# Two attention layers on one core: 64x128 products in place of 64x64 quadrants, and another order at the end of a batch

## The chip, the core and the metric

The kernel runs on one core of a Trainium2 chip. The metric is the device time of one execution in microseconds; the kernel before takes 5070.74 us (median of three runs, 5064.38 to 5071.53). The profile shown here is of an execution with a span of 5060.0 us. The engines are called PE (TensorE, the matrix engine; its weight loads are listed apart as PEld), DVE (VectorE), ACT (ScalarE), POOL (GpSimd) and SP (SyncE, which issues most of the transfers). All data are 32-bit floats.

## What is computed

The input is an array of 8 images, 512 channels by 1024 positions. Two layers of attention with residuals run one after the other. Layer 0 is ordinary attention of 8 heads with 64 channels each, and the change leaves it alone. Layer 1, cut to what matters:

```python
q, k, v = (einsum("oc,bct->bot", w, gn(x)) for w in (w_q, w_k, w_v))  # 8 heads of 64
attn = einsum("bhdq,bhdT->bhqT", q, k) * scale           # "scores"
attn = einsum("gh,bhqT->bgqT", w_head, attn)             # "mixing": heads are mixed
attn = softmax(attn, axis=-1)
mean, var = attn.mean((-2, -1)), attn.var((-2, -1))      # one pair a batch and head
attn = (attn - mean) / sqrt(var + EPS) * in_gamma + in_beta
out = einsum("bhqT,bhdT->bhqd", attn, v)                 # "values"
x = x + w_proj @ out + b_proj
```

Mixing stands between the scores and the exponential, so it must be done on all 8 heads' scores of a query and key. The division by the softmax's sum, and the normalisation over a whole head (the "instance" statistics), are applied to the result instead of to the 1024 x 1024 weights: the kernel needs sums of e and of e squared for each query and head, and scales `out` with them.

## The kernel before

The order of the instructions on each engine is the order in which the program emits them (a manual schedule), and each engine takes its queue in order. Waits between engines are put in by the framework where data or buffers demand them.

Layer 1 works through the batches one by one. One batch has 4 query blocks of 256 queries and 4 key blocks of 256 keys, so 16 blocks `t`, and two *half-steps* `x` for each: `half_step` (L1302 on) is called for x = 0 to 36. In a half-step x below 32 the scores of four heads are made, in two parts `i`; mixing lags four half-steps behind (`y = x - MLAG`), and squares, sums and values lag five (`w = y - 1`). So in the steady part, x = 5 to 31, PE does in this order: scores part 0, mix j = 0 and 1, scores part 1, values.

- `scores(x, i)` (L1117) makes 2 heads x 256 queries x 256 keys into a PSUM tile of two banks, index m (the head) choosing the bank. The tile `s` has one buffer; for x below 4 two of three parts use the tiles `m` instead, of which there are two. The result is copied to `raw` in SBUF (L1126 by DVE, L1128 by ACT), one of the two being chosen by i and x.
- `regroup(t)` (L1137), after an odd x, sends `raw` to eight tiles `re` by SP's transfers, so that the heads of one query come to lie on neighbouring partitions.
- `mix(y, j)` (L1150) multiplies pieces of `re` as the stationary operand with the constant `wmix`, 64 columns: 32 products for each j, 8 tiles `re` (R_ORDER) by 2 halves of the keys (`c`) by 2 halves of the partitions (`a`). The result is in a tile `m`; ACT takes its exponential (L1156). `c` selects the half of the output's partitions, `a` the partitions of the inputs and the PSUM bank.
- `squares` (L1166, ACT), `sum_e` and `sum_e2` (L1171, L1173, L1177, DVE) gather the sums.
- `values(w)` (L1195) adds to two accumulators in PSUM.
- After every eighth values block, `totals` (L1221) sums over the keys with a product by ones, PE; the rows are copied by DVE and ACT (L1232, L1230) and brought to a compact form `c` by two transfers (L1236). `leave` (L1210, L1212) copies the accumulators out. `reciprocals` (L1244 to L1264) inverts the sums, sends them to DRAM (`zd`, L1246) and back, broadcast to all partitions (`rzb`, L1249), and adds up the squares; `divide` (L1270) multiplies by `rzb`. For the first three query blocks the last two are run 2 and 5 half-steps later, from an agenda.
- While half-steps 32 to 35 run, two `k_half` each (L1004) make the next batch's keys.

After the last half-step come `leave`, the first pair of the next batch's V projection (`v_pair`, PE, L1021, copied by ACT L1025 and then DVE L1026), the flushed agenda with `reciprocals` and `divide` of the last query block, `instance` (which sums the squares, L1276 and L1278, spreads the sum by a small product `pi` on PE, L1280, and takes an inverse root by a chain of small DVE operations, L1282 to L1292), the second V pair, `affine` for 8 heads (L1298 ACT, L1300 DVE), the output product (L1083) and the next batch's queries (L1053). `small_psum1` and `v_pair` both take their PSUM from the two buffers of `m`.

Of the kernel before, what the change touches and what calls it, by code (L numbers as in the profile page):

```python
# [18 lines left out]
P = 128  # L19
# [448 lines left out]
def tile_two_attention_layers(  # L468
# [19 lines left out]
    nc = tc.nc  # L488
    B, C, T = x_d.shape
    H = w_head.shape[0]  # L490
    D = C // H
# [24 lines left out]
    def const_tile(name, shape, dt=F32):  # L516
        return const.tile(shape, dt, tag=name, name=name)
# [13 lines left out]
    ones = const_tile("ones", [P, P])  # L531
# [12 lines left out]
    wmix = const_tile("wmix", [P, H, Q8])  # L544
# [26 lines left out]
    NQB = 4  # L571
# [78 lines left out]
    with ExitStack() as l0:  # L650
# [42 lines left out]
        for oc in range(3 * NCC):  # L693
            for c in range(NCC):
                nc.tensor.matmul(
                    pbq[:, oc : oc + 1], w0[:, c, ts(oc, P)], gnb[:, c : c + 1],
                    start=(c == 0), stop=(c == NCC - 1),
# [5 lines left out]
        n_t, xa_t, q_t, k_t, v_t = {}, {}, {}, {}, {}  # L703
# [187 lines left out]
        for b in range(B):  # L891
            ag = Agenda()
# [25 lines left out]
    with ExitStack() as l1:  # L918
# [16 lines left out]
        KB = 2 * P  # L935
# [4 lines left out]
        MLAG = 4  # L940

        def m_psum(nm):
            return ps_m.tile([P, 2, FB], F32, tag="m", name=nm)

        def small_psum1(nm):
            return m_psum(nm)[:, 0]

        y_t, qo_t, k_t, v_t, w_t = {}, {}, {}, {}, {}
# [64 lines left out]
        def v_pair(b, i):  # L1013

            if i == 0:
                v_t[b] = kvpool.tile([P, NT, C], F32, tag="v", name=f"v1_{b}")
            ps = m_psum(f"pv1_{b}_{i}")
            w = w_t["v", b]
            for m in range(2):
                for c in range(NCC):  # L1020
                    nc.tensor.matmul(  # L1021
                        ps[:, m], y_t[b][:, c, ts(2 * i + m, P)], w[:, c],
                        start=(c == 0), stop=(c == NCC - 1),
                    )
            nc.scalar.copy(v_t[b][:, 2 * i], ps[:, 0])  # L1025
            nc.vector.tensor_copy(v_t[b][:, 2 * i + 1], ps[:, 1])  # L1026
# [71 lines left out]
        class Attention1:  # L1098
# [4 lines left out]
            def scores(self, x, i):  # L1103

                b, t, hp = self.b, x // 2, x % 2 * 2 + i
                qb, kb = t // NKB, t % NKB
                nm = f"s1_{b}_{x}_{i}"
                if x < MLAG and (2 * x + i) % 3:
                    ps = m_psum(nm)
                else:  # L1110
                    ps = ps_s.tile([P, 2, FB], F32, tag="s", name=nm)
                pv = ps.rearrange("p m (j k) -> p m j k", j=2)
                for j in range(2):
                    for c in range(2):
                        for m in range(2):
                            r = slice(m * D, m * D + D)
                            nc.tensor.matmul(  # L1117
                                pv[c * D : c * D + D, m, j],
                                qo_t[b][r, 2 * qb + j, hp, ts(c, D)],
                                k_t[b][r, hp, ts(kb, KB)], start=True, stop=True,  # L1120
                            )
                if x % 2 == 0 and i == 0:
                    self.raw[t] = rawpool.tile([P, H, 2, KB], F32, tag="raw", name=f"raw_{b}_{t}")
                dst = self.raw[t][:, 2 * hp : 2 * hp + 2]
                if i == 0 and (x < MLAG or x % 2 == 0):
                    nc.vector.tensor_copy(dst, pv)  # L1126
                else:
                    nc.scalar.copy(dst, pv)  # L1128
# [10 lines left out]
            def mix(self, y, j):  # L1139

                t, kc = y // 2, y % 2
                if j == 0:
                    self.e[y] = epool.tile([P, 2, T], F32, tag="e", name=f"e1_{self.b}_{y}")
                ps = m_psum(f"m1_{self.b}_{y}_{j}")
                for r in R_ORDER:
                    for c in range(2):
                        k0 = kc * P + c * D
                        for a in range(2):
                            rows = slice(a * D, a * D + D)
                            nc.tensor.matmul(  # L1150
                                ps[c * D : c * D + D, a, ts(r, D)],
                                self.re[t, r][rows, j, k0 : k0 + D],
                                wmix[rows].rearrange("p g i -> p (g i)"),
                                start=True, stop=True,
                            )
                nc.scalar.activation(self.e[y][:, j], ps.rearrange("p a c -> p (a c)"), AF.Exp)  # L1156

            def squares(self, y, j):
# [113 lines left out]
            def instance(self):  # L1272

                b = self.b
                s = stat.tile([P, 1], F32, tag="is", name=f"is_{b}")
                nc.vector.reduce_sum(s, self.s2, axis=AX.X)  # L1276
                sb = stat.tile([P, H], F32, tag="isb", name=f"isb_{b}")
                nc.vector.tensor_scalar_mul(sb, blk8, s)  # L1278
                ps = small_psum1(f"pi_{b}")
                nc.tensor.matmul(ps[:, :H], ones, sb, start=True, stop=True)  # L1280
                var = stat.tile([P, H], F32, tag="ivar", name=f"ivar_{b}")
                nc.vector.tensor_scalar(  # L1282
                    var, ps[:, :H], 1.0 / (T * T), EPS - 1.0 / (T * T), ALU.mult, ALU.add
                )
                r = rsqrt(stat, var, f"i_{b}", H)
                self.A = stat.tile([P, H], F32, tag="iA", name=f"iA_{b}")
                nc.vector.tensor_mul(self.A, r, gam8)
                self.cv = stat.tile([P, H], F32, tag="icv", name=f"icv_{b}")
                nc.vector.scalar_tensor_tensor(
                    self.cv, self.A, -1.0 / T, bet8, ALU.mult, ALU.add  # L1290
                )
                nc.vector.tensor_mul(self.cv, self.cv, vs[:, :, b])  # L1292
# [9 lines left out]
            def half_step(self, x, ag):  # L1302
                y, w = x - MLAG, x - MLAG - 1
                if 0 <= w - 1 < NX and w % QLAG == 0:
                    self.leave((w - 1) // QLAG)
                if 0 <= w < NX:
                    self.squares(w, 0)
                    self.sum_e(w, 0)
                if x < NX:
                    self.scores(x, 0)  # L1310
                if 0 <= w < NX:
                    self.squares(w, 1)
                    self.sum_e(w, 1)
                    self.sum_e2(w, 0)
                    self.sum_e2(w, 1)
                if 0 <= y < NX:
                    self.mix(y, 0)
                    self.mix(y, 1)
                if x < NX:
                    self.scores(x, 1)  # L1320
                    if x % 2:
                        self.regroup(x // 2)
                if 0 <= w < NX:
                    self.values(w)
                    self.e.pop(w)
                    if w % QLAG == QLAG - 1:
                        qb = w // QLAG
                        self.totals(qb)
                        ag.at(x + 2, lambda: self.reciprocals(qb))
                        ag.at(x + 5, lambda: self.divide(qb))  # L1330
                ag.run(x)


# [15 lines left out]
        for b in range(B):  # L1349
            more = b + 1 < B  # L1350
            a = Attention1(b)
            ag = Agenda()
            for i in range(NV):
                ag.at(1, lambda i=i: v_pair(b, NV + i))
            if more:
                for c in range(NCC):
                    ag.at(6 + 2 * c, lambda c=c: load_y(b + 1, [c]))
                    ag.at(14 + 2 * c, lambda c=c: load_w(("k", b + 1), wkT, [c]))
                    ag.at(22 + 2 * c, lambda c=c: load_w(("v", b + 1), wvT, [c]))
                    ag.at(24 + c, lambda c=c: normalize1(b + 1, [c]))  # L1360
                for i in range(2 * NCC):
                    ag.at(NX + i // 2, lambda i=i: k_half(b + 1, i))
            for x in range(NX + MLAG + 1):
                a.half_step(x, ag)

            a.leave(NQB - 1)
            if more:
                v_pair(b + 1, 0)
            ag.flush()
            a.instance()  # L1370
            if more:
                load_w(("q", b + 1), wqT)
                v_pair(b + 1, 1)
            for g in range(H):
                a.affine(g)
            for oc in range(NCC):
                out1(b, oc)
            if more:
                for oc in range(NCC):
                    q_chunk(b + 1, oc)  # L1380
# [69 lines left out]
```

## Time and profile before

| | busy us | share of the span | instructions |
|---|---|---|---|
| PE | 4542.6 | 90% | 58392 |
| PEld | 2440.7 | 48% | 58392 |
| DVE | 2643.7 | 52% | 3082 |
| ACT | 2008.8 | 40% | 2161 |
| POOL | 271.7 | 5% | 139 |

Layer 0 fills the time up to about 2050 us, layer 1 the rest, some 373 us a batch. Each product of 32-bit floats stands in the trace as two matmuls and two weight loads, so that the counts are twice the program's. A busy time is the union of the instructions of a group; the mean that follows it is the length of one, and since several run at once on different parts of the array, the sum of the lengths is larger. "Idle before" is the idle time of the engine just before the instructions of a group, with what ended it; "issue" means that nothing in the profile explains it. A form like `64*64 64x256` reads: 64 rows and 64 columns of weights, and an output of 64 partitions by 256 columns. In the tables by window the columns are the length, the busy time and count of PE, PEld, DVE, ACT and POOL, the granted PE clock, the share of the DMA engines and GB/s. Matmuls may be missing from a trace, a few per cent at most, and their ends are modelled, so that starts are the better measure.

### The profile page before, as it was taken

The page shows a single profiled execution, that of the slowest core. Times are in us where ns is not written, and L with a number is a line of the kernel's source. Part 1 is how long each engine was busy: PE and PEld are TensorE (multiplying, and loading weights), DVE is VectorE, ACT ScalarE, POOL GpSimd, SP SyncE. Part 2 cuts the span into 40 slices and gives each one's busy share as a digit, 9 for nine tenths or more (in the row PEclk, how much of TensorE's full clock was granted, in tenths as well). Part 3 has the DMA queues.
Part 4 walks back from the last instruction along what each step waited for, and adds up shares of the span by engine and source line. Part 5 has one row for each costly group of instructions (what it writes and reads, how often), then busy time and mean ns, then how long its engine had stood idle before and what let it go on. Part 6 is the DMA issues. An engine that isn't in the chain of part 4 may idle for free.

```text
span 5060.0 us, 128186 instructions
## 1 busy us (share of the span) xinstructions
PE 4542.6 (90%) x58392; PEld 2440.7 (48%) x58392; DVE 2643.7 (52%) x3082; ACT 2008.8 (40%) x2161; POOL 271.7 (5%) x139
## 2 busy tenths in 40 slices
PE   7999999999999999988888888888888888888987
PEld 4343424242424243466366466466465465465464
DVE  1737373838283828266265266266275265265365
ACT  0414141404141414076176175165175265274274
POOL 1202020202020200000000000000000000000000
PEclk9999999999999999999999999999999999999999
DMA  1000000000000000265264264264274364363364
GB/s 67 1 33 1 34 1 34 1 33 1 34 1 34 1 17 0 84 173 129 64 178 121 76 170 119 81 164 119 85 177 102 101 163 100 100 174 99 100 149 111
DMA packets 205048, 408.68 MB, mean 81 GB/s; under 512 B 35024, under 2 KB 35024, under 8 KB 204496
## 3 DMA queue, kind: packets, MB, share of 16 engines
q1 hardware_dynamic: 203072, 396.19, 29.1%
q8 instruction: 458, 7.50, 0.7%
q10 hardware_dynamic: 1152, 4.19, 0.2%
q14 instruction: 94, 0.77, 0.1%
q0 software_dynamic: 272, 0.02, 0.0%
HBM read 97.54 MB, written 33.82 MB: 26 GB/s over the span
## 4 chain that ended last, share of the span: by engine, by line
PE 81%; DVE 6%; issue 5%; ACT 5%; DMA 2%; SPq 0%; DVEq 0%; ACTq 0%
PE a L1195 9%; PE s L1117 9%; PE s L820 8%; PE m L1150 8%; PE a L845 8%; PE pv L1021 5%; PE pp L1083 5%; PE pk L1004 5%; PE pk L768 4%; PE pq L1053 4%; PE pp L768 4%; PE pq L768 4%; PE pv L791 4%; PE t L1221 2%; ACT raw L1128 1%
## 5 line engine op out<-in xcount | busy, mean ns | idle before, releaser
L825 ACT ACTIVATE e<-s 128x1024 f32<-128x1024 f32 x512 | 498.6, 1022 | 568.2 <-PE s L820 557.2
L1150 PE MATMUL m<-wmix,re 64*64 64x64 f32 x32768 | 561.9, 219 | 123.1 <-issue 115.6
L1117 PE MATMUL s<-k,q 64*64 64x256 f32 x8192 | 575.7, 389 | 86.9 <-issue 48.1
L1150 PEld LDWEIGHTS m<-wmix,re 64*64 64x64 f32 x32768 | 544.2, 135 | 178.0 <-issue 140.1
L1173 DVE TENSOR_TENSOR z<-z,e 128x1024 f32<-128x1024 f32 x448 | 536.6, 1219 | 123.4 <-ACT e L1156 123.3
L1195 PE MATMUL a<-e,v 128*64 128x128 f32 x8192 | 550.9, 288 | 49.4 <-issue 49.4
L1156 ACT ACTIVATE e<-m 128x1024 f32<-128x1024 f32 x512 | 504.3, 1024 | 200.2 <-PE m L1150 199.4
L1177 DVE TENSOR_TENSOR z<-z,e 128x1024 f32<-128x1024 f32 x448 | 532.1, 1220 | 62.4 <-ACT e L1166 61.7
L1195 PEld LDWEIGHTS a<-e,v 128*64 128x64 f32 x8192 | 478.3, 144 | 161.7 <-issue 159.5
L820 PE MATMUL s<-q,k 64*128 64x512 f32 x2048 | 523.5, 629 | 2.3
L845 PE MATMUL a<-e,v 128*64 128x512 f32 x2048 | 495.2, 605 | 0.0
L1166 ACT ACTIVATE e<-e 128x1024 f32<-128x1024 f32 x448 | 461.5, 1069 | 0.0
L1128 ACT COPY raw<-s 128x1024 f32<-128x1024 f32 x368 | 373.7, 1015 | 198.4 <-PE s L1117 190.3
L833 DVE TENSOR_TENSOR zacc<-zacc,e 128x1024 f32<-128x1024 f32 x320 | 411.5, 1286 | 48.0 <-ACT e L825 24.2
L1117 PEld LDWEIGHTS s<-k,q 64*64 64x64 f32 x8192 | 288.7, 134 | 243.7 <-issue 113.0
L1126 DVE COPY raw<-s 128x1024 f32<-128x1024 f32 x144 | 176.3, 1224 | 308.4 <-PE s L1117 286.5
L820 PEld LDWEIGHTS s<-q,k 64*128 64x128 f32 x2048 | 178.3, 189 | 327.6 <-issue 168.4
L845 PEld LDWEIGHTS a<-e,v 128*64 128x64 f32 x2048 | 125.1, 136 | 343.8 <-issue 324.9
L858 DVE RECIPROCAL rz<-z 128x512 f32<-128x512 f32 x64 | 214.8, 3356 | 81.0 <-PE z L854 81.0
L1083 PE MATMUL pp<-q,wp 128*128 128x512 f32 x512 | 231.9, 615 | 21.5 <-DVE q L1300 16.8
L1021 PE MATMUL pv<-wv,y 128*128 128x512 f32 x512 | 243.9, 635 | 0.0
L1004 PE MATMUL pk<-y,wk 128*128 128x512 f32 x512 | 231.3, 606 | 5.9 <-DMA y<-x 5.9
(165 smaller groups left out, 3547.4 us busy)
## 6 DMA issues: line engine op xcount, KB each, us to landing
re<-raw SPq DMA_DIRECT2D x1024, 256.0 KB
x<-in_x_dram SPq DMA_DIRECT2D x32, 512.0 KB
x<-x SPq DMA_DIRECT2D x32, 512.0 KB
y<-x SPq DMA_DIRECT2D x32, 512.0 KB
rzb<-zd SPq DMA_DIRECT2D x64, 256.0 KB
xs<-x SPq DMA_DIRECT2D x32, 512.0 KB
out_dram<-xs SPq DMA_DIRECT2D x32, 512.0 KB
wk<-in_wkT_dram SPq DMA_DIRECT2D x32, 256.0 KB
```

Of the source, the lines that this page charges most:

```text
L768: nc.tensor.matmul(ps[:, f], w[:, c, o0 + oc * P : o0 + (oc + 1) * P], rhs[:, c, ts(f, FB)], start=(c == 0), stop=(c == NCC - 1),)
L820: nc.tensor.matmul(ps[:, m], k[r, hp, ts(kc, P)], q[r, hp, ts(f, FB)], start=True, stop=True,)
L825: nc.scalar.activation(e[i], ps, AF.Exp)
L845: nc.tensor.matmul(acc[g][m * D : m * D + D], v[:, kc, ts(2 * hp + m, D)], e[i][:, m], start=(kc == 0), stop=(kc == NG - 1),)
L1021: nc.tensor.matmul(ps[:, m], y_t[b][:, c, ts(2 * i + m, P)], w[:, c], start=(c == 0), stop=(c == NCC - 1),)
L1083: nc.tensor.matmul(ps[:, f], w[:, n, ts(oc, P)], out_view(b)[:, n, ts(f, FB)], start=(n == 0), stop=(n == NQB - 1),)
L1117: nc.tensor.matmul(pv[c * D : c * D + D, m, j], qo_t[b][r, 2 * qb + j, hp, ts(c, D)], k_t[b][r, hp, ts(kb, KB)], start=True, stop=True,)
L1150: nc.tensor.matmul(ps[c * D : c * D + D, a, ts(r, D)], self.re[t, r][rows, j, k0 : k0 + D], wmix[rows].rearrange("p g i -> p (g i)"), star ...
L1156: nc.scalar.activation(self.e[y][:, j], ps.rearrange("p a c -> p (a c)"), AF.Exp)
L1173: nc.vector.tensor_add(self.z[:, j], self.z[:, j], self.e[y][:, j])
L1177: nc.vector.tensor_add(self.z2[:, j], self.z2[:, j], self.e2[j])
L1195: nc.tensor.matmul(self.acc[w][j * D : j * D + D, s].rearrange("p (c i) -> p c i", i=Q8), v_t[b][:, kc, ts(g, D)], self.by_head(self.e[y][ ...
```

## The change

It has three parts, all in layer 1. Scores and mixing no longer split the output's partitions into two halves: a product takes 64 rows and 128 columns of weights in place of two with 64 columns, so that there are half as many instructions. The DVE's share of the evictions of scores in the steady part moves from even half-steps to odd ones, where only ACT evicted. At the end of a batch the last `reciprocals` comes directly after `leave`, ahead of the V pair, and `instance` is cut in two: the sums before the V pair, the product and the root after it; `divide` and `affine` follow, and the second V pair is emitted after them. The aim is fewer instructions on PE and a shorter chain between the last values and the output product.

```diff
                 for j in range(2):
-                    for c in range(2):
-                        for m in range(2):
-                            r = slice(m * D, m * D + D)
-                            nc.tensor.matmul(
-                                pv[c * D : c * D + D, m, j],
-                                qo_t[b][r, 2 * qb + j, hp, ts(c, D)],
-                                k_t[b][r, hp, ts(kb, KB)], start=True, stop=True,
-                            )
+                    for m in range(2):
+                        r = slice(m * D, m * D + D)
+                        nc.tensor.matmul(
+                            pv[:, m, j], qo_t[b][r, 2 * qb + j, hp],
+                            k_t[b][r, hp, ts(kb, KB)], start=True, stop=True,
+                        )
...
-                if i == 0 and (x < MLAG or x % 2 == 0):
+                if i == 0 and (x < MLAG or x % 2):
                     nc.vector.tensor_copy(dst, pv)
...
                 for r in R_ORDER:
-                    for c in range(2):
-                        k0 = kc * P + c * D
-                        for a in range(2):
-                            rows = slice(a * D, a * D + D)
-                            nc.tensor.matmul(
-                                ps[c * D : c * D + D, a, ts(r, D)],
-                                self.re[t, r][rows, j, k0 : k0 + D],
-                                wmix[rows].rearrange("p g i -> p (g i)"),
-                                start=True, stop=True,
-                            )
+                    for a in range(2):
+                        rows = slice(a * D, a * D + D)
+                        nc.tensor.matmul(
+                            ps[:, a, ts(r, D)], self.re[t, r][rows, j, ts(kc, P)],
+                            wmix[rows].rearrange("p g i -> p (g i)"),
+                            start=True, stop=True,
+                        )
...
                 nc.vector.tensor_scalar_mul(sb, blk8, s)
+                self.sb = sb
+
+            def instance_end(self):
+                b = self.b
                 ps = small_psum1(f"pi_{b}")
-                nc.tensor.matmul(ps[:, :H], ones, sb, start=True, stop=True)
+                nc.tensor.matmul(ps[:, :H], ones, self.sb, start=True, stop=True)
...
                         self.totals(qb)
-                        ag.at(x + 2, lambda: self.reciprocals(qb))
-                        ag.at(x + 5, lambda: self.divide(qb))
+                        if qb < NQB - 1:
+                            ag.at(x + 2, lambda: self.reciprocals(qb))
+                            ag.at(x + 5, lambda: self.divide(qb))
...
             a.leave(NQB - 1)
+            a.reciprocals(NQB - 1)
+            a.instance()
+            ag.flush()
             if more:
                 v_pair(b + 1, 0)
-            ag.flush()
-            a.instance()
+            a.instance_end()
+            a.divide(NQB - 1)
+            for g in range(H):
+                a.affine(g)
             if more:
                 load_w(("q", b + 1), wqT)
                 v_pair(b + 1, 1)
-            for g in range(H):
-                a.affine(g)
             for oc in range(NCC):
                 out1(b, oc)
```

## The prediction

> **What bounds the kernel now.** The slices of the page come first: TensorE (PE) is busy in tenths 8 or 9 all along, so I look for what its time in layer 1 is made of. The costliest groups, and the DMA queues for one line:
>
> ```profile
> L1150 PE MATMUL m<-wmix,re 64*64 64x64 f32 x32768 | 561.9, 219 | 123.1 <-issue 115.6
> L1117 PE MATMUL s<-k,q 64*64 64x256 f32 x8192 | 575.7, 389 | 86.9 <-issue 48.1
> L1195 PE MATMUL a<-e,v 128*64 128x128 f32 x8192 | 550.9, 288 | 49.4 <-issue 49.4
> ...
> q8 instruction: 458, 7.50, 0.7%
> ```
>
> Mixing (L1150), scores (L1117) and values (L1195) each take some 560 us, and before them PE stands idle for 115.6 + 48.1 + 49.4 = 213 us on "issue", which no semaphore explains. The timeline of PE over two half-steps of batch 3 shows where:
>
> ```profile
> 3288.69 1.09 PE L1117 MATMUL s<-k,q 64*64 64x256 f32 x16
> 3289.61 2.04 PE L1150 MATMUL m<-wmix,re 64*64 64x64 f32 x128
> 3291.47 1.05 PE L1117 MATMUL s<-k,q 64*64 64x256 f32 x16
> 3292.45 1.97 PE L1195 MATMUL a<-e,v 128*64 128x128 f32 x32
> 3294.34 1.09 PE L1117 MATMUL s<-k,q 64*64 64x256 f32 x16
> 3295.26 2.04 PE L1150 MATMUL m<-wmix,re 64*64 64x64 f32 x128
> 3297.12 0.61 PE L1117 MATMUL s<-k,q 64*64 64x256 f32 x7
> 3300.35 0.86 PE L1117 MATMUL s<-k,q 64*64 64x256 f32 x9 [2.62 <-issue]
> ```
>
> An undisturbed half-step is, start to start, 0.92 (scores) + 1.86 (mix) + 0.98 (scores) + 1.89 (values) = 5.65 us; PE waits for no eviction in it. But in the second one it halts within a score block, after 7 of 16 products. A half-step has 192 records of matmuls and as many weight loads, 384 instructions, 256 of them in the 1.86 us of the mix. In the trace's DMA records packets of the instruction queue (16 KB each: 7.50 MB / 458) start at 3297.81 and 3313.92 us, where PE has just halted (last start before the halt near 3297.4), and PE goes on about 1.4 us after each has landed; when PE starves they follow each other 3.6 us apart. So I read the halt as instruction fetch. The third view, windows, gives its side effect and a warning for later:
>
> ```profile
> 2102.20:2106.00 3.80, 3.80 (x130) 3.78 (x129) 0.69 (x1) 0.59 (x1) 0.00 (x0) 1.00 0.00 0
> 2106.60:2110.00 3.40, 3.40 (x6) 1.34 (x5) 0.00 (x0) 0.00 (x0) 0.00 (x0) 0.50 0.00 0
> 3284.60:3300.30 15.70, 13.13 (x384) 10.38 (x384) 10.30 (x9) 10.53 (x11) 0.00 (x0) 0.90 0.68 171
> ```
>
> The granted clock (third column from the right) falls with the halts. Counted from the first to the 27th values block of a batch (26 half-steps and three blocks of totals of 3.03 us), the timelines give 188.6 to 203.0 us, mean 196.2 for batches 0 to 6 and 190.9 for the last: 7.2 us a half-step, not 5.65. ACT has 5.5 us of work in one (L1156 504.3, L1166 461.5 + 68.6, L1128 373.7, over 256), DVE 5.0, so neither bounds it.
>
> Last, the end of a batch, PE and the DMA issues:
>
> ```profile
> 3155.76 1.97 PE L1195 MATMUL a<-e,v 128*64 128x128 f32 x32
> 3160.72 2.96 PE L1221 MATMUL t<-z,ones 128*32 128x512 f32 x8 [3.00 <-DVE z L1177]
> ...
> 3166.34 8.02 PE L1021 MATMUL pv<-wv,y 128*128 128x512 f32 x16
> 3184.03 0.56 PE L1280 MATMUL pi<-isb,ones 128*128 128x8 f32 x2 [9.66 <-DVE isb L1278]
> 3184.45 9.19 PE L1021 MATMUL pv<-wv,y 128*128 128x512 f32 x16
> 3196.05 1.52 PE L1083 MATMUL pp<-q,wp 128*128 128x512 f32 x3 [2.40 <-DVE q L1300]
> ...
> 3167.09 1.21 SPq L1236 DMA_DIRECT2D c<-row  x2
> 3175.90 0.33 SPq L1246 DMA_DIRECT2D zd<-rz  x1
> 3177.32 1.14 SPq L1249 DMA_DIRECT2D rzb<-zd  x2
> ```
>
> The reciprocals sit behind the eviction of the V pair on DVE, the little product pi behind the divide and its broadcast from DRAM, and the second V pair behind pi: 9.66 us idle, then a cold clock. From the last values block to the output product takes 38.8 us on average in batches 0 to 6, 24.4 in batch 7.
>
> **What the Trainium skill says.** "TensorE: Matmul & The Clock Gate", LDWEIGHTS: a load takes columns / 1.2 ns, whatever the rows: 53 ns for 64 columns, 107 for 128. The trace agrees:
>
> ```profile
> 2102.15 3.81 PEld L1038 LDWEIGHTS pvs<-ys,wv 128*64 128x64 f32 x128 [0.76 <-issue]
> 1005.27 0.30 PEld L820 LDWEIGHTS s<-q,k 64*128 64x128 f32 x4 [0.81 <-ACT e L825]
> ```
>
> 128 loads of 64 columns in two column halves, with products of only 8 columns, come as pairs 58.3 ns apart: load-bound, 53 + 5. The four loads of a layer 0 score (64 rows, 128 columns) span 0.30 us with 0.19 each, so the second pair starts 0.11 after the first, and two row halves load together. Same page, HAM clock gate: a window of 3.4 us with little activity halves the clock; here that followed the idle of 2.6 us and more, and the load-bound stretch at 2102 (the windows above). "Runtime: NRT & Kernel Launch", instruction fetch: blocks of 16 KiB, 256 instructions, boundaries "mostly hidden". The packets agree in size; hidden they are not where a block is used up in 1.9 us. "TensorEngine Tiling (Array Packing)": row tiles run in parallel if they write different PSUM banks; the layer 0 pairs do, and m and a index banks here too.
>
> **The change, part by part.**
> *Scores.* Half as many products, of 128 columns and 256 long. Pairs at the 215.5 ns that the quadrants show now, four pairs instead of four fours: the same 0.86 us; the first load of a block is exposed for 0.05 more. 0.97 + 0.98.
> *Mix.* 64 loads of 128 columns in 32 pairs, products of 64 columns. The product streams 53 ns, the load needs 107: load-bound, 107 + 5 = 112 ns a pair (bounds: 109, the first pair of layer 0; 165 if load and product of the same rows could not overlap, 107 + 53 + 5). I take 112, as the layer 0 pairs and the load-bound v_sums say: 32 x 0.1117 = 3.57 us instead of 1.86, +1.71. It is on PE's path.
> *Fetch.* A half-step falls to 224 instructions; the fastest stretch, the mix, uses 128 in 3.57 us, 36 per us, half of 256 in 3.6 us. The halts and their cold windows go. Half-step: 0.97 + 3.57 + 0.98 + 1.89 = 7.41 us.
> *Evictions.* The DVE eviction moves from even to odd half-steps. ACT then has 6.0 us in an even one (two exps, two squares, two copies) and 5.0 in an odd one, DVE 4.3 and 5.6: under 7.41, so nothing. Behind ACT's second copy waits the next score block, 1.89 us of values later; the copy ends about 2.3 us after the mix, the block starts at 2.87.
> *Sums per batch* (0 to 6). Steady part 26 x 7.41 + 3 x 3.03 = 201.8 against 196.2: +5.6. First mix to first values: 3.57, then two exps and a copy on ACT until 5.9, then 5.5: 11.4 against 9.1, +2.3. The last five half-steps, where the next keys' projection (7.1 us) stands between: four mixes of 3.79 with the drain. Now one takes 2.03 and three 2.56, 47.5 in all where nothing halts, which would be +5.4; the mean with halts is 50.05, so 52.9 is +2.8.
> *End of a batch.* The reciprocals no longer wait for the V pair: the trace of batch 7, where there is none, gives 1.86 us from the issue of c to them, 1.4 from zd to rzb, 4.7 to the divide. So isb is ready at 3170.2, under the first V pair. Pi follows that pair at once (3174.4). The second V pair now waits for the PSUM buffer of the first, free at 3175.7 after the copies by ACT and DVE. DVE: pi's chain 3.0 us to 3178.7, the divide to 3179.9 (broadcast landed 3175.4), two affines per engine to 3181.5, all beside the V pair, which ends PE's queue at 3182.9. New waits: DVE's reciprocals wait 1.9 us for c with only that copy queued behind, whose PE work lasts longer. The V copies now wait behind the affines, which PE needs only 6.9 us later. Tail 24.4 instead of 38.8 (one cold block of totals aside): -14.4, and the output product starts warm, 27.7 instead of 28.9: -1.2.
> Sum: 5.6 + 2.3 + 2.8 - 15.6 = -4.9, seven times: -34. Batch 7: 201.8 - 190.9 = +10.9, +2.6, +0.1, and a tail in which only instance and its root (4.1) move under the broadcast: +9.5. Total about -24: 5070.7 - 24 = 5046.
>
> **Rivals.**
> *Trade, 0.80:* the above, 5046. Two gains of different kind meet an equal loss. Each ns of the pair's spacing is 32 x 32 x 8 ns = 8 us; 109 gives 5024, 115 gives 5073; the tail is good for 20 either way.
> *Weight loads worse, slower, 0.11:* a spacing of 125 gives 4.0 us a mix, +0.43 x 256 = 110: 5155; 165 gives 5480. For it: mixing would stream products only half the time, and the load-bound stretch at 2102 was followed by half clock. Against: there products streamed a tenth of it.
> *Halts stay, slower, 0.02:* if they are not the fetch, 7.41 + 1.5: about 5360.
> *Loads of 64 rows cost half, faster, 0.07:* the mix stays at 1.9, ACT's 6.0 bounds the half-step: -1.4 x 256, 4690. Against: the 0.11 us of layer 0.
>
> **How the numbers follow.** In the first case faster by over 0.2% (10 us) has 0.70, within 0.18, slower 0.12. With the others: faster 0.63, same 0.15, slower 0.22. The range 4995 to 5120 takes in the first case with its bounds and a spacing of 120, and leaves out 0.2.
>
> **What would show it.** Mix blocks of x64 lasting 3.57 us start to start (1.9 or 5 refutes the loads); no "issue" before L1146 and L1116; values to values 7.4; clock 1.00 in the steady part; pi without a wait, and 24 us from the last values to the output product.

## The result, and the profile after

The changed kernel takes 5034.99 us (median of four runs, 5034.15 to 5035.81), the kernel before 5067.56 us in the same comparison (5061.06 to 5071.53). The ratio is 0.9937, with a 95% interval of 0.992 to 0.9954: 32.6 us faster. The prediction was 5046 us, between 4995 and 5120. The profiled spans are 5060.0 us before and 5033.6 us after.

The groups of the page of the changed kernel that answer to those shown of before, and the queue of the instructions (columns: busy time, mean ns of one, then the idle time before them and what ended it):

```profile
L1146 PE MATMUL m<-wmix,re 64*128 64x64 f32 x16384 | 946.7, 271 | 0.0
L1116 PE MATMUL s<-k,q 64*128 64x256 f32 x4096 | 559.4, 395 | 15.3 <-ACT raw L1126 8.9
L1190 PE MATMUL a<-e,v 128*64 128x128 f32 x8192 | 503.5, 276 | 0.0
...
q8 instruction: 298, 4.88, 0.4%
```

The 213 us of "issue" are gone from all three groups, as predicted; the scores cost about what they cost before (559.4 us busy, 575.7 with twice the instructions); and mixing, with half the instructions, is busy for 946.7 us in place of 561.9. The timeline of PE over a half-step and a half of the steady part (start, length, instructions) shows what it is made of:

```profile
3276.15 1.97 PE L1190 MATMUL a<-e,v 128*64 128x128 f32 x32
3278.05 1.14 PE L1116 MATMUL s<-k,q 64*128 64x256 f32 x8
3279.02 3.68 PE L1146 MATMUL m<-wmix,re 64*128 64x64 f32 x64
3282.53 1.09 PE L1116 MATMUL s<-k,q 64*128 64x256 f32 x8
3283.55 1.97 PE L1190 MATMUL a<-e,v 128*64 128x128 f32 x32
3285.45 1.14 PE L1116 MATMUL s<-k,q 64*128 64x256 f32 x8
```

Start to start: 0.97 + 3.51 + 1.02 + 1.90 = 7.40 us, without a gap, and the same in every half-step. A window of the steady part shows PE busy for 99.19 of 100 us, at the full granted clock of 1.00 (columns as explained with the profile before):

```profile
3050.00:3150.00 100.00, 99.19 (x1258) 79.44 (x1258) 56.85 (x61) 58.33 (x63) 0.00 (x0) 1.00 0.48 118
```

The end of the batch whose end the prediction showed, PE:

```profile
3161.34 1.97 PE L1190 MATMUL a<-e,v 128*64 128x128 f32 x32
3166.30 2.96 PE L1216 MATMUL t<-z,ones 128*32 128x512 f32 x8 [3.00 <-DVE z L1172]
3170.06 1.06 PE L1216 MATMUL t<-z,ones 128*32 128x512 f32 x8 [0.79 <-DVE row L1227]
3171.06 7.13 PE L1021 MATMUL pv<-wv,y 128*128 128x512 f32 x16
3178.03 0.28 PE L1279 MATMUL pi<-isb,ones 128*128 128x8 f32 x2
3179.59 7.13 PE L1021 MATMUL pv<-wv,y 128*128 128x512 f32 x16 [1.28 <-DVE v L1026]
3186.56 4.03 PE L1083 MATMUL pp<-q,wp 128*128 128x512 f32 x9
```

Of the 9.66 us before `pi` nothing is left. In their place PE waits 1.28 us for the copies of the first V pair, and the output product starts 25.22 us after the last values block, at full speed.

The parts of a batch that the change touches, from the two traces, in us. They are counted from start to start, the output product by its own length; before and after are means of batches 0 to 6, which are followed by another batch:

| part | before | after | predicted after |
|---|---|---|---|
| first mix to first values | 9.07 | 11.22 | 11.4 |
| first to 27th values (26 half-steps, three totals) | 196.23 (188.6 to 203.0) | 200.98 (every batch) | 201.8 |
| 27th to last values (next keys between) | 50.05 | 52.62 | 52.9 |
| last values to output product | 38.80 | 25.32 | 24.4 |
| output product | 28.87 | 27.63 | 27.7 |

The rows sum to 323.02 and 317.77 us, so a batch gains 5.25 us, and seven of them 36.7. The last batch, from its own rows, loses 10.1 us in its steady part (190.88 to 200.98) and 2.4 before it, and gains only 4.4 at its end (22.62 to 18.20 from the last values block to the output product): 8.3 lost, with its two small rows. (The 24.4 us that the prediction reads for this batch count from the last block but one, which the timeline merges with the last; none of its sums uses them.) 36.7 - 8.3 = 28.4 us, against 26.4 between the two spans. The other 2 us lie outside the table: layer 1 reaches its first mix 1.2 us later, and the queries and first scores take 50.91 us a batch in place of 50.79. So the products lose and the end of the batch wins, which the medians alone do not tell. The experiments take the two apart.

### The profile page after: what moved, and what is told of

Same layout as the page of the kernel before. It is cut to its first block, busy times and chain, and to the rows that moved or that the text cites. A ratio compares the mean times of both kernels' runs of the same rounds, so it can differ in the third digit from the quotient of the medians.

```text
span 5033.6 us, 87202 instructions
## 1 busy us (share of the span) xinstructions
PE 4840.6 (96%) x37912; PEld 2881.8 (57%) x37912; DVE 2653.2 (53%) x3082; ACT 2027.2 (40%) x2161; POOL 271.8 (5%) x139
## 4 chain that ended last, share of the span: by engine, by line
PE 92%; DVE 6%; ACT 1%; DMA 1%; issue 0%; DVEq 0%; SPq 0%
PE m L1146 18%; PE s L1116 10%; PE a L1190 9%; PE s L820 8%; PE a L845 8%; PE pk L1004 5%; PE pv L1021 4%; PE pk L768 4%; PE pp L1083 4%; PE pq L1053 4%; PE pp L768 4%; PE pq L768 4%; PE pv L791 4%; PE t L1216 2%; DVE zacc L833 1%; PE z L854 1%
## 5 line engine op out<-in xcount | busy, mean ns | idle before, releaser
L1146 PEld LDWEIGHTS m<-wmix,re 64*128 64x128 f32 x16384 | 954.0, 188 | 27.6 <-issue 17.8
L1146 PE MATMUL m<-wmix,re 64*128 64x64 f32 x16384 | 946.7, 271 | 0.0
L1151 ACT ACTIVATE e<-m 128x1024 f32<-128x1024 f32 x512 | 523.1, 1022 | 336.6 <-PE m L1146 336.6
L1116 PE MATMUL s<-k,q 64*128 64x256 f32 x4096 | 559.4, 395 | 15.3 <-ACT raw L1126 8.9
L1190 PE MATMUL a<-e,v 128*64 128x128 f32 x8192 | 503.5, 276 | 0.0
L1190 PEld LDWEIGHTS a<-e,v 128*64 128x64 f32 x8192 | 441.9, 137 | 78.9 <-issue 76.8
L1116 PEld LDWEIGHTS s<-k,q 64*128 64x128 f32 x4096 | 357.7, 187 | 112.9 <-issue 63.8
L845 PEld LDWEIGHTS a<-e,v 128*64 128x64 f32 x2048 | 125.3, 136 | 344.0 <-issue 325.0
L1021 PE MATMUL pv<-wv,y 128*128 128x512 f32 x512 | 226.6, 599 | 8.9 <-DVE v L1026 8.9
L768 PE MATMUL pk<-n,w 128*128 128x512 f32 x512 | 226.2, 601 | 7.1 <-DVE n L737 7.1
```

What stands on the lines that cost most here:

```text
L768: nc.tensor.matmul(ps[:, f], w[:, c, o0 + oc * P : o0 + (oc + 1) * P], rhs[:, c, ts(f, FB)], start=(c == 0), stop=(c == NCC - 1),)
L845: nc.tensor.matmul(acc[g][m * D : m * D + D], v[:, kc, ts(2 * hp + m, D)], e[i][:, m], start=(kc == 0), stop=(kc == NG - 1),)
L1116: nc.tensor.matmul(pv[:, m, j], qo_t[b][r, 2 * qb + j, hp], k_t[b][r, hp, ts(kb, KB)], start=True, stop=True,)
L1146: nc.tensor.matmul(ps[:, a, ts(r, D)], self.re[t, r][rows, j, ts(kc, P)], wmix[rows].rearrange("p g i -> p (g i)"), start=True, stop=True,)
L1190: nc.tensor.matmul(self.acc[w][j * D : j * D + D, s].rearrange("p (c i) -> p c i", i=Q8), v_t[b][:, kc, ts(g, D)], self.by_head(self.e[y][ ...
```

## The experiments

The theory under test has four parts: (a) the mix is now bound by its weight loads, 128 columns each; (b) what vanished are halts of PE for instruction fetch, which depend on how many instructions PE uses per us; (c) the gain is that of the shorter chain at the end of a batch, and adds to the loss of the products; (d) the order of the evictions is worth nothing. The main rival is that the products themselves bring a gain, through the halts or through a better order of evictions.

### The two parts apart

One kernel has the new end of a batch alone, with the products and evictions of before:

```diff
 # kernel before, with only
...
             a.leave(NQB - 1)
+            a.reciprocals(NQB - 1)
+            a.instance()
+            ag.flush()
             if more:
                 v_pair(b + 1, 0)
-            ag.flush()
-            a.instance()
+            a.instance_end()
+            a.divide(NQB - 1)
+            for g in range(H):
+                a.affine(g)
...
```

> The new end of a batch alone; scores and mixing stay in quadrants, evictions stay as before. Theory (the gain is at the batch's end, and the steady part of the changed kernel gives some of it back): 7 batch ends of about 13.5 us less idle and 1.2 us less of a cold output product, and 4 us at the last, so 5067 - 107 = 4960 us, faster than the changed kernel; values to values stays at 7.2 us on average with halts on issue. Rival (the fewer instructions make the gain, the new end is hidden): 5055 to 5070 us.

The other has the products and the evictions, with the old end:

```diff
 # kernel before, with only
-                    for c in range(2):
-                        for m in range(2):
+                    for m in range(2):
...
-                if i == 0 and (x < MLAG or x % 2 == 0):
+                if i == 0 and (x < MLAG or x % 2):
...
-                    for c in range(2):
-                        k0 = kc * P + c * D
-                        for a in range(2):
+                    for a in range(2):
...
```

> The 64x128 products and the other order of evictions alone, with the old end of a batch. Theory: the steady part becomes regular at 7.4 us a half-step and costs 9.5 us a batch more, 12 in the last, so 5067 + 79 = 5146 us, slower than before; no halts on issue in the steady part, and a gap of some 10 us before pi at the end of each batch. Rival (fewer instructions make the gain): 5035 to 5050 us.

The end alone: 4953.54 us, ratio 0.9777 (0.9749 to 0.9805). The products alone: 5143.06 us, ratio 1.0163 (1.0135 to 1.0192). Their product, 0.9777 x 1.0163 = 0.9936, is the 0.9937 of the change: the two parts add up. The end of a batch with quadrants, from the first V pair on, PE:

```profile
3141.19 8.37 PE L1021 MATMUL pv<-wv,y 128*128 128x512 f32 x16
3149.40 0.28 PE L1284 MATMUL pi<-isb,ones 128*128 128x8 f32 x2
3150.97 7.13 PE L1021 MATMUL pv<-wv,y 128*128 128x512 f32 x16 [1.28 <-DVE v L1026]
3157.94 27.63 PE L1083 MATMUL pp<-q,wp 128*128 128x512 f32 x64
```

The chain is the same as in the changed kernel: `pi` without a wait, then 1.28 us. So the change holds a gain of 2.2% and a loss of 1.6%, and the half of it that was to save instructions is the half that costs. Which of the moves at the end of a batch brings how much was not tried.

### Is the mix bound by its weight loads?

Each mixing product is made to stream 128 columns in place of 64, with the same loads. The second half repeats the constant and writes over the result of the next tile, so this changes what is computed.

```diff
 # changed kernel, with
+                        c0 = min(r, NR - 2) * D
...
-                            ps[:, a, ts(r, D)], self.re[t, r][rows, j, ts(kc, P)],
-                            wmix[rows].rearrange("p g i -> p (g i)"),
+                            ps[:, a, c0 : c0 + 2 * D].rearrange(...),
+                            self.re[t, r][rows, j, ts(kc, P)],
+                            wmix[rows].unsqueeze(1).to_broadcast([D, 2, H, Q8]),
...
```

> The changed kernel with 128 columns streamed in each mixing product instead of 64, same weights, so a product streams for 107 ns instead of 53; the second 64 columns repeat the first and overwrite a neighbour's, so the mixed scores of part of the queries are not those of the reference. Theory (the mix is bound by its weight loads of 107 ns): a block of 64 products stays at 3.5 to 3.6 us, the time within 0.5% of 5035 us. Rival (load and product of a pair add up): 107 more than 53 on top, 5.2 us a block, 5035 + 1.7 x 256 = 5470 us.

It takes 5036.11 us (one run), next to 5034.99. The timeline of PE:

```profile
3279.81 3.74 PE L1147 MATMUL m<-wmix,re 64*128 64x128 f32 x64
3283.38 1.03 PE L1116 MATMUL s<-k,q 64*128 64x256 f32 x8
```

The mix takes 3.57 us start to start with twice the streamed columns, against 3.51; the half-step is 7.40 again. Within a block the pairs of products start 112 ns apart in both kernels, as their weight loads do. Only the second pair of a block follows the columns streamed: it starts 57 ns after the first in the changed kernel and 109 ns here, which is the whole difference. The number of instructions doesn't set the time either, for the quadrants put twice as many through in 1.86 us, with fours 58 ns apart. So columns streamed are nearly free here and columns loaded set the time: part (a) holds.

### The order of the evictions

```diff
 # changed kernel, with
-                if i == 0 and (x < MLAG or x % 2):
+                if i == 0 and (x < MLAG or x % 2 == 0):
```

> The changed kernel with the old order of evictions (DVE takes its share in even half-steps). Theory (both orders fit under a half-step of 7.4 us): within 0.2% of 5035 us, values to values unchanged. Rival (the new order is needed, since ACT would be late in odd half-steps): slower by 0.5% or more, with waits of the scores for ACT's copies.

5037.81 us (5032.51 to 5039.23), and the steady part is 200.98 us in every batch, as after the change. Part (d) holds: the parity is worth nothing that can be measured.

### Scores and mix, each in both forms

Wide scores with the mix in quadrants:

```diff
 # changed kernel, with
-                    for a in range(2):
+                    for c in range(2):
+                        k0 = kc * P + c * D
+                        for a in range(2):
...
-                            ps[:, a, ts(r, D)], self.re[t, r][rows, j, ts(kc, P)],
+                                ps[c * D : c * D + D, a, ts(r, D)],
+                                self.re[t, r][rows, j, k0 : k0 + D],
...
```

> The changed kernel with the mixing alone put back into quadrants (64 columns of weights); scores stay 64x128. 352 instructions a half-step instead of 224 or 384, 256 of them in the mix's 1.9 us. Theory (instruction fetch in blocks of 256, a block used up in under 3.6 us makes PE halt): the loads get cheap again, 5.8 us of PE work, but the halts come back, about one of 2.5 us in two half-steps or a little fewer, so 6.9 to 7.1 us a half-step and 4920 to 4960 us. Rival (the halts came from the scores in quadrants or from the old evictions): no halts, 5.8 to 6.0 us a half-step, about 4650 us.

Scores in quadrants with the wide mix:

```diff
 # changed kernel, with
-                    for m in range(2):
+                    for c in range(2):
+                        for m in range(2):
...
-                            pv[:, m, j], qo_t[b][r, 2 * qb + j, hp],
+                                pv[c * D : c * D + D, m, j],
+                                qo_t[b][r, 2 * qb + j, hp, ts(c, D)],
...
```

> The changed kernel with the scores alone put back into quadrants; the mix stays 64x128. Theory (a score block of 256 columns costs the same in both forms, and 256 instructions a half-step with 128 in 3.5 us make no halt): within 0.3% of 5035 us. Rival (the wide scores carry part of the gain): slower by 0.5% or more, or halts on issue.

With the changed kernel and the first experiment (whose evictions have the parity that is worth nothing) this makes a square, all with the new end of a batch:

| | mix in quadrants | wide mix |
|---|---|---|
| scores in quadrants | 4953.54 | 5097.44 (ratio 1.0056, 1.0039 to 1.0074) |
| wide scores | 4867.48 (ratio 0.9626, 0.9594 to 0.9659) | 5034.99 |

The wide mix costs 144 us in the upper row and 168 in the lower, the wide scores bring 86 and 62. The better half of the products is the scores: with them alone, and the new end, the kernel is 4867.48 us.

Both numbers missed what was expected of them. The first is 1% below its range; the second is 1.2% above the changed kernel, which was the sign of its rival: the wide scores do carry a part of the gain. The timeline of the first, PE:

```profile
3230.88 1.13 PE L1116 MATMUL s<-k,q 64*128 64x256 f32 x8
3231.95 2.10 PE L1148 MATMUL m<-wmix,re 64*64 64x64 f32 x128
3233.97 1.13 PE L1116 MATMUL s<-k,q 64*128 64x256 f32 x8
3235.04 1.97 PE L1193 MATMUL a<-e,v 128*64 128x128 f32 x32
```

With the next block of scores at 3236.93, an undisturbed half-step is 6.05 us there, more than the 5.65 of quadrants throughout. It was below the expectation all the same, because halts are fewer: the idle time on "issue" before mixing is

```profile
L1148 PE MATMUL m<-wmix,re 64*64 64x64 f32 x32768 | 557.6, 220 | 65.7 <-issue 58.5 <-DVE k L1011 6.5
```

half of before's 115.6 (the averages follow in the table on halts below). The timeline of the second, PE:

```profile
3306.05 3.79 PE L1148 MATMUL m<-wmix,re 64*128 64x64 f32 x64
3309.77 1.09 PE L1117 MATMUL s<-k,q 64*64 64x256 f32 x16
3310.79 1.97 PE L1192 MATMUL a<-e,v 128*64 128x128 f32 x32
3312.69 1.09 PE L1117 MATMUL s<-k,q 64*64 64x256 f32 x16
```

Nothing halts in it, and its half-step is 1.02 (the first scores, from 3305.03) + 3.72 + 1.02 + 1.90 = 7.66 us, 0.26 longer than the changed kernel's, though scores in quadrants alone are no slower. What it has more of is changes of the shape of tile: four in a half-step (scores 64 x 64, mix 64 x 128, scores, values 128 x 64) where the changed kernel has two, because its scores and mix share one shape. 0.26 / 2 = 0.13 us for a change. The trace shows where it goes: the second pair of a mix starts 160 ns after the first, in place of 57, and the scores start 208 ns after the last pair, in place of 112. The wide scores with a quadrant mix have four changes too, and 6.05 us in place of 5.65.

### A third form: half of the mix in each shape

Here the mix for j = 0 is in quadrants and for j = 1 wide, so that a half-step has 288 instructions, between 352 (the wide scores with a quadrant mix) and 224 (the changed kernel).

```diff
 # changed kernel, with
+                if j == 0:
+                    ...  (quadrants, as in the kernel before)
+                else:
                     for r in R_ORDER:
                         for a in range(2):
...
```

> The changed kernel with mix j = 0 in quadrants (64 columns of weights) and mix j = 1 in 64x128 as it is. 288 instructions a half-step; any 256 in a row take at least 4.6 us. Theory (loads of 128 columns cost 1.76 us a mix against 0.93, and a block of 256 instructions that lasts more than some 4 us makes no halt): no halts, 7.40 - 0.82 = 6.57 us a half-step, 32 mixes of 8 batches times 0.82 us less, 5035 - 210 = 4825 us. Rival (the halts depend on the quadrants themselves): halts of some 1 to 2.5 us again, 7.0 us or more a half-step, 4900 to 5000 us.

4916.68 us (4915.38 to 4917.4), ratio 0.9698 (0.9675 to 0.972): 92 us above the expectation and within the range of its rival, halts that stay. The trace tells the two apart. PE:

```profile
3244.27 1.13 PE L1116 MATMUL s<-k,q 64*128 64x256 f32 x8
3245.34 1.16 PE L1149 MATMUL m<-wmix,re 64*64 64x64 f32 x64
3246.43 2.00 PE L1159 MATMUL m<-wmix,re 64*128 64x64 f32 x32
3248.26 1.09 PE L1116 MATMUL s<-k,q 64*128 64x256 f32 x8
3249.28 1.97 PE L1203 MATMUL a<-e,v 128*64 128x128 f32 x32
```

The halts are gone, as expected: no "issue" stands before the mix, and the steady part is 188.13 us in every batch but the first (188.82). The miss is in the half-step: 1.07 + 1.09 + 1.83 + 1.02 + 1.90 (to the next scores at 3251.18) = 6.91 us in place of 6.57, again with four changes of shape: 0.17 us for each of the two that are new.

### Spreading the mix over the half-step

If halts come from using 256 instructions faster than they are fetched, then a half-step with as many instructions, but with its dense block split, should halt less. The values block is cut in two, and mixing and values alternate:

```diff
 # wide scores with the mix in quadrants (above), with
-            def values(self, y):
+            def values(self, y, part):
...
-                for g in range(H):
+                for g in range(4 * part, 4 * part + 4):
...
                     self.mix(y, 0)
-                    self.mix(y, 1)
+                if 0 <= w < NX:
+                    self.values(w, 0)
                 if x < NX:
                     self.scores(x, 1)
...
+                if 0 <= y < NX:
+                    self.mix(y, 1)
                 if 0 <= w < NX:
-                    self.values(w)
+                    self.values(w, 1)
...
```

> Scores 64x128, mixing in quadrants, new end, and PE's order in a half-step changed to scores 0, mix 0, values of heads 0 to 3, scores 1, mix 1, values of heads 4 to 7: the same 352 instructions as in e3, but no more than 160 of them in less than 1.9 us. Theory (a halt comes where a block of 256 is used up faster than the next is fetched, 3.6 us or a little more): few or no halts, 5.8 to 6.1 us a half-step, bound by ACT's 6.0 in even ones, so 4640 to 4720 us. Rival (the number of instructions alone counts, 352 a half-step): halts as in e3, 6.8 us a half-step, 4860 us or more.

The same order of PE with scores in quadrants too:

> As e8 (scores 0, mix 0, values of heads 0 to 3, scores 1, mix 1, values of heads 4 to 7), but the scores in quadrants too: 384 instructions a half-step, and 4 changes of the tile's shape in it instead of 6. Theory (two costs: fetch of blocks of 256, floor 3.6 us a block and some 4 to 5 us as it comes, and 0.1 us or a little more for each change of shape): 5.8 us without halts, with more halts than e8, since a block lasts 3.9 us: 6.2 to 6.6 us a half-step, 4790 to 4880 us. Rival (what cost e8 its 6.36 us a half-step is the split itself): 6.4 us and the halts on top, 4900 us or more.

And the same order with scores and mix both wide, as in the changed kernel:

> The changed kernel (all products 64x128) with PE's order of e8: 224 instructions a half-step, so no halts, and 4 changes of shape (64x128 to 128x64 and back, twice) instead of 2. Theory (a change of shape costs 0.1 us or a little more): half-step 7.6 to 7.7 us instead of 7.40, 5080 to 5120 us. Rival (a change of shape costs nothing, e9 and e6 lost their time otherwise): 7.4 us, 5030 to 5040 us.

The first takes 4835.16 us (4831.36 to 4843.89), ratio 0.9541 (0.9517 to 0.9566), the fastest of all these kernels and faster than both before and after, though well short of the 4640 to 4720 expected. The second takes 4885.21 us, ratio 0.9636 (0.9604 to 0.9668), just above its expectation and below its rival's 4900; the third 5085.34 us, ratio 1.0033 (1.0023 to 1.0042), within it. PE in the first, half a half-step and the start of the next half:

```profile
3218.35 1.14 PE L1116 MATMUL s<-k,q 64*128 64x256 f32 x8
3219.42 1.16 PE L1148 MATMUL m<-wmix,re 64*64 64x64 f32 x64
3220.51 1.09 PE L1193 MATMUL a<-e,v 128*64 128x128 f32 x16
3221.53 1.14 PE L1116 MATMUL s<-k,q 64*128 64x256 f32 x8
```

1.07 + 1.09 + 1.02 = 3.18 us for half a half-step, 6.36 for a whole one, with six changes of shape; that is what the expectation had left out. "Issue" before mixing is down to 33.2 us (its group) with as many instructions as in the kernel that has 58.5. The second has 384 instructions in a half-step; the group of its mix, and PE over half a half-step:

```profile
L1150 PE MATMUL m<-wmix,re 64*64 64x64 f32 x32768 | 617.9, 220 | 106.7 <-issue 105.7
...
3251.76 1.09 PE L1117 MATMUL s<-k,q 64*64 64x256 f32 x16
3252.67 1.11 PE L1150 MATMUL m<-wmix,re 64*64 64x64 f32 x64
3253.71 1.09 PE L1195 MATMUL a<-e,v 128*64 128x128 f32 x16
3254.73 1.09 PE L1117 MATMUL s<-k,q 64*64 64x256 f32 x16
```

So its undisturbed half-step is shorter (0.91 + 1.04 + 1.02 us for a half by these lines, 5.96 for a whole one), with four changes of shape, and it is slower as a whole, for its halts. And PE in the third:

```profile
3301.78 1.13 PE L1116 MATMUL s<-k,q 64*128 64x256 f32 x8
3302.75 1.90 PE L1146 MATMUL m<-wmix,re 64*128 64x64 f32 x32
3304.57 1.09 PE L1190 MATMUL a<-e,v 128*64 128x128 f32 x16
3305.60 1.13 PE L1116 MATMUL s<-k,q 64*128 64x256 f32 x8
```

0.97 + 1.82 + 1.03 = 3.82, 7.64 us for a half-step: 0.24 more than the changed kernel for two more changes of shape, with the same instructions: 0.12 us for a change, since only the order of PE differs. The order alone also differs between 6.36 and 6.05 us (scores wide, mix in quadrants) and between 5.96 and 5.65 (quadrants throughout), and there a change costs 0.15. In these three pairs a half-step also has two blocks more. With the scores in quadrants and the mix wide it has none more and pays 0.13 all the same, so the cost goes with the shape.

### The halts against the packets

The table takes every gap of over 0.75 us between the starts of neighbouring matmuls of PE in layer 1, and counts as halts those with a packet of the instruction queue (16 KB) that started no earlier than 2 us before the gap and landed, as the last one, within 2 us before its end. The last two columns are the shortest and the mean half-step of the steady part, without those that have a block of totals:

| kernel | instructions a half-step, order | halts with such a packet | sum of the gaps, us | shortest, us | mean, us |
|---|---|---|---|---|---|
| before | 384 | 153 | 272 | 5.65 | 7.26 |
| new end alone | 384 | 155 | 274 | 5.65 | 7.29 |
| quadrants, split turns | 384, spread | 117 | 169 | 5.96 | 6.93 |
| wide scores, quadrant mix | 352 | 84 | 143 | 6.05 | 6.88 |
| wide scores, quadrant mix, split turns | 352, spread | 50 | 62 | 6.36 | 6.72 |
| half of the mix wide | 288 | 11 | 16 | 6.90 | 6.91 |
| scores in quadrants, wide mix | 256 | 14 | 17 | 7.66 | 7.66 |
| changed kernel | 224 | 9 | 12 | 7.40 | 7.40 |
| changed kernel, split turns | 224, spread | 11 | 15 | 7.64 | 7.64 |

The 9 to 14 at the bottom are at least in part other waits beside which a packet happened to land (the gap at 3168.2 in the changed kernel ends with the copy of the totals' row), and in these four kernels no "issue" stands before the matmuls of the mix. In the kernels above them, PE goes on at a median of 1.41 to 1.47 us after the landing (10% to 90%: 1.0 to 1.7 us), and only one packet in twenty follows the one before it sooner than about 3.6 us.

The number of packets fits PE's instructions: 2 x 58392 matmuls and loads before are 456 times 256, and the queue has 458 packets; 2 x 37912 after are 296 times 256, with 298 packets. And a packet takes no longer beside a halt than elsewhere (median 1.22 us beside a halt and 1.19 us over all of layer 1, kernel before), so the halts do not come with packets that are slow in themselves. This is the pattern of an engine that waits for its instructions, and the count falls with their number and, at equal number, with their spreading. No run delayed the fetch by itself, so (b) is supported by a count in nine kernels rather than shown by a cause.

## Why the prediction was right

**Weight loads of the mix.** Right: the pairs start 112 ns apart, as taken, and the streaming of 128 columns shows that it is the loads. A mix is 0.06 us shorter than 32 times that, because its second pair doesn't wait for a load.

**Scores.** The cost of the first block, 0.97 us, is what was predicted; the second is 1.02, not 0.98. The two misses of 0.04 and 0.06 nearly cancel, which is why the half-step of 7.40 agrees so well with 7.41; that much is luck. Most of the 0.8 us that the steady part lies below the predicted 201.8 is in the blocks of totals: the prediction took 3.03 us for each, about their mean before with the halts in it, and undisturbed they take 2.88 both before and after.

**Fetch.** Right: no "issue" before the scores and the mix, a clock of 1.00 in the steady part, and the same time in every batch. The profile's mean clock goes from 0.971 to 0.989.

**Evictions at nothing.** Right, and tested by turning them back.

**End of a batch.** The chain ran as worked out: the first part of `instance` is done at 3175.02 (L1273, DVE), 3.0 us before PE needs it; `pi` is without a wait; DVE's chain from the product to `divide` takes 2.9 us (L1281 at 3179.46 to L1265 at 3182.35), 3.0 predicted. The prediction's 24.4 us, however, has both blocks of totals and the V pair at full clock. Of the seven batches one has that, 24.35 us; five have a first block of totals at half clock (0.50 from 3166.30 to 3169.30 in the batch shown) after PE's wait for DVE's sums, 0.8 to 0.9 us more; one is slower still, 26.89. In the mean, 25.32. The cold block that the prediction set aside is not the exception but the rule.

The new waits cost what was said, the 1.28 us of PE for the first V pair, and no more. The work of ACT and DVE beside the second V pair is hidden, with the margin that was worked out. Their affines and V copies in the trace of the changed kernel, and below them the start of the output product in the critical chain of the kernel before:

```profile
3182.35 1.22 DVE L1265 TENSOR_TENSOR q<-q,rzb 128x1024 f32<-128x1024 f32 x1
3183.60 1.91 DVE L1299 TENSOR_SCALAR q<-q,iA,icv 128x512 f32<-128x512 f32 x4
3187.38 0.69 DVE L1026 COPY v<-pv 128x512 f32<-128x512 f32 x1 [1.86 <-ACT v L1025]
...
3183.66 2.93 ACT L1297 ACTIVATE q<-q,icv,iA 128x512 f32<-128x512 f32 x4 [4.85 <-DVE q L1265]
3186.76 0.58 ACT L1025 COPY v<-pv 128x512 f32<-128x512 f32 x1 [0.17 <-PE pv L1021]
...
3194.91 1.00 DVE q L1300 x2
...
3196.05 4.10 PE pp L1083 x9
```

For its first eight matmuls, on 512 of the 1024 positions, the output product needs two affines of each engine; in the kernel before it starts after two of DVE's four. In the changed kernel ACT's first two end at 3185.18 (1.52 us after 3183.66) and DVE's before them, 1.4 us ahead of the product's start at 3186.56; the prediction had 1.4 us. ACT's fourth ends at 3186.59, and the eight matmuls that need it start only some 3.4 us after the first. So PE's own queue sets the end of a batch here, not this chain. The V copies wait for PE (0.17 us on `pv`) and not for the affines before them.

**The sum.** Per batch -5.25 us where -4.9 was predicted, +8.3 for the last where +9.5 was: -28.4 in place of -24. The number agrees better than its terms, since the steady part costs 0.8 us a batch less than predicted and the end brings 0.9 us less. The medians differ by 32.6, so of the 11 us between 5046 and 5035 some 3 are the base (5070.7 there, 5067.56 here), and the rest the gain.

**The rivals.** Loads that cost more (125 ns and up) and loads at half price are both refuted by the 112 ns. The halts did not stay. For the first of these the prediction had also pointed at the clock, because the mix would stream for only about half of its time; the clock stays at 1.00.

What no rival said is that the change could be split. The working had it all the same: -15.6 for the end of each batch, with -4.1 in the last one, is -113 us, and +10.7 for the rest, with +13.6 in the last one, is +88. The end alone measured -0.0223 x 5066 = -113, the products alone 0.0163 x 5066 = +83 (5066 us is the kernel before in that comparison).

## What to carry to other kernels

Before a product is widened to halve the instructions, compare the columns that its weights load with those that it streams: where the load is the longer, two narrow products that load side by side can be the faster form, as 58 ns against 112 here for products that stream 64 columns. Where PE halts on "issue", count its instructions against the packets of its queue, and first try to spread the dense block among sparse ones, or to thin out a neighbour whose products stream long. When a change has independent parts, price and run them apart: here one part alone is 1.6% better than the sum.

## What the runs showed of the hardware that was not expected

A change of the shape of tile between neighbouring blocks costs PE 0.12 to 0.17 us: 0.24 us a half-step for two more in the changed kernel with split turns, 0.26 for two more with scores in quadrants, 0.31 for two more where split turns meet a mix in quadrants, 0.34 with the half-wide mix. The Trainium skill, "TensorEngine Tiling (Array Packing)", Key Properties, says that changing the tiling mode drains TensorE, and gives no time; the traces agree that there is a cost, but whether it is a drain was not tested. It was missing from four expectations, by up to 0.34 us a half-step in the half-wide mix (6.91 against 6.57), and it takes part of the gain of the fastest kernel, which has six in a half-step.

By the count above, though by no run that delayed it, the fetch of instructions is behind the 213 us of "issue" before mixing, scores and values in the kernel before, 4% of its span. The Trainium skill, "Runtime: NRT & Kernel Launch", Instruction fetch mechanics, calls the crossing of a block's boundary mostly hidden; here it was not. The halts had vanished at 288 instructions in 6.91 us, and were there at 352 in 6.36.
